# Layer 1 of a two-layer graph network: masks on 64x64 tiles, six two-head steps on VectorE, and a group's divisions three steps apart

## The chip, the cores and the metric

The kernel runs on one core of one Trainium2 chip. The metric is the device time of one execution in microseconds (us). Five engines of the core matter: TensorE (PE in the profile, its weight loads PEld), VectorE (DVE), ScalarE (ACT), GpSimd (POOL) and SyncE (SP), which here only issues transfers. Each engine works through its own queue in order; they meet at semaphores.

## What is computed

Layer 0 is dense attention with an additive bias taken from the adjacency matrix. Layer 1, which the change concerns, is a graph attention with 8 heads of 64 features over 4096 nodes. Cut to what matters:

```python
h = relu(layernorm(x))
nX = per_head_layernorm((h @ W).reshape(n, 8, 64)).transpose(1, 0, 2)
at1 = einsum('kno,ok->kn', nX, a1)[:, :, None]
at2 = einsum('kno,ok->kn', nX, a2)[:, :, None]
kg = leaky_relu(at1 + at2.transpose(0, 2, 1), 0.2) * graph      # 8 x 4096 x 4096
mg = where(mask, kg, -32768.0)
y = softmax(mg, -1) @ nX + nX
x = x + elu(y.transpose(1, 0, 2).reshape(n, 512))
```

`graph` is the float matrix and `mask` says where it is not zero. Both belong to a node pair and are the same for all heads.

## The kernel before

**Tiling of layer 1.** All is held transposed: sources on the 128 partitions, targets in the free dimension. A *group* is 512 targets (`ic`, 8 of them) times four heads (`hg`, 2 of them): 16 groups. A group walks over the sources in 32 *steps* of 128 (`jt`), so there are 512 steps. Four steps share one set of loads, a *block* (`JB = 4`). A step handles four heads of 128 x 512 logits each: heads 0 and 1 are one PSUM tile of two banks (`pair[0]`), heads 2 and 3 another (`pair[1]`). These tiles have the tag `d` and rotate over three buffers; two further banks, `acc0` and `acc1`, hold the group's sums.

**One step** n goes through these functions, with the engine and the line of the profile:

- `z_sums` (PE): four small matmuls with six contracted rows each, on row tiles of 32, put the two-sided logit into PSUM (L1069); then four matmuls of the identity with `ng`, the bf16 mask tile (0 or -2^60), add the mask to each head (L1074). The order is heads 2, 3, 0, 1.
- `relu` (ACT, L1081) makes part of the leaky relu of heads 0 and 1.
- `leaky` (DVE): two `scalar_tensor_tensor` on heads 3 and 2 (L1091), one product with the graph values g (L1096) for the heads that VectorE multiplies itself, and one addition for heads 0 and 1 (L1097). VectorE multiplies head 3 alone, or heads 2 and 3 in a step that is in the set `light`.
- `weigh` (POOL, L1104): the product with g for the other three heads, or for two in a step of `light`.
- `exponent` (ACT, L1107): exp of all four heads.
- `values` (PE, L1120): the weights times the features, on two column tiles of 64. The last column of the features is ones, which gives the softmax sum.

The loop runs them skewed: in iteration n come `values(n - 4)`, `exponent(n - 3)`, `leaky(n)`, `weigh(n)`, `z_sums(n + 1)`, `relu(n + 1)`. The logit tile `t` has six buffers.

**A group's end.** When `values` has done jt = 31, `finish` spreads the rest of the group over the next group's iterations, by a list of offsets d from the iteration n (which is 3 modulo 32) and a place in it: `copies` (ACT, PSUM sums to SBUF, L1136), `to_rows(hf)` (PE, eight records per half, L1142, into one more tile of tag `d`), `divide(hf)` (DVE: reciprocal L1151, product L1153, addition of `own` into `y` L1154), then on ACT `minus`, `exps`, `positive`, `less_one`, and on POOL `elu` (L1178) and `close` (L1182), whose result is stored. `own` (the features that are added) and `xi` (the residual) are loaded by `load_rows`.

**Order.** A call wrapped in `seq` keeps its place in its engine's queue as the program writes it. Row loads and output stores are not wrapped; the framework places them. `load_adj(q)` issues a block's loads on SP: `z2` (128 KB), `nb` (the masks, 512 KB) and `g` (1 MB), two buffers each. In the first group the last 512 rows are still being prepared for layer 1 (`make_ready`), and in the first four groups POOL makes `own` once each (L365, L366).

Of the kernel before, what the change touches and what calls it, by code (L numbers as in the profile page):

```python
# [10 lines left out]
F32 = mybir.dt.float32  # L11
BF16 = mybir.dt.bfloat16
# [6 lines left out]
P = 128  # L19
N = 4096  # L20
D = 512
NH = 8
HD = 64
NB = N // P
SB = 4
# [10 lines left out]
GC = 512  # L36
# [42 lines left out]
def fast_path(  # L79
# [18 lines left out]
    nc = tc.nc  # L98
    seq = tc.keep_in_program_order
# [13 lines left out]
    const = ctx.enter_context(tc.tile_pool(name="const", bufs=1))  # L113
# [4 lines left out]
    ident_b = const.tile([P, P], BF16, name="ident_b")  # L118
# [24 lines left out]
    nT_d = dram.tile([NB, P, N], BF16, name="nT_d")  # L143
# [30 lines left out]
        return mv  # L174


    aa = [const.tile([P, NH, HD], F32, name=f"a{e}_sb") for e in (1, 2)]
    aln_sb = const.tile([P, HD], F32, name="aln_sb")
    bln2_sb = const.tile([P, HD], F32, name="bln2_sb")
    at_b = const.tile([P, 2, NH], F32, name="at_b")  # L180
# [284 lines left out]


    with tc.tile_pool(name="early", bufs=2) as early, tc.tile_pool(name="kv", bufs=1) as kv:
        v = kv.tile([P, NB, D], F32, name="v")
        TILES = [(ic, jt) for ic in range(NI) for jt in range(NB)]
        n_tiles = len(TILES)  # L470
# [66 lines left out]
        with tc.tile_pool(name="proj_c", bufs=1) as pc, tc.tile_pool(  # L537
            name="proj", bufs=2
# [216 lines left out]
            for k in range(KC):  # L755
                pa_ps = psum.tile([P, 512], F32, name="pa", tag="mm", bufs=2)
                for c in range(SB):
                    seq(nc.tensor.matmul(
                        pa_ps, turned["q"][:, c, ts(k, P)], turned["k"][:, c, :],
                        start=c == 0, stop=c == SB - 1,  # L760
# [10 lines left out]
            for sb in range(1, NS):  # L771
                if sb + 2 < NS:
                    xts[sb + 2] = load_x(sb + 2)
                if sb == 1:
                    seq(nc.sync.dma_start(
                        out=w1_sb.rearrange("p k h e -> p k (h e)"),
                        in_=w1.rearrange("(k p) o -> p k o", p=P),
# [23 lines left out]
        with tc.tile_pool(name="attn", bufs=2) as work, tc.tile_pool(  # L801
            name="attn_ps", bufs=2, space=PSUM
# [142 lines left out]
            for s in range(0, n_tiles, 2):  # L945
                ic, jt = TILES[s]
# [48 lines left out]
    with tc.tile_pool(name="ga_in", bufs=2) as inputs, tc.tile_pool(  # L995
# [4 lines left out]
        JB = 4  # L1000
# [3 lines left out]
        inverses = gat.tile([P, NI, 2, 2, 2, 4], F32, name="inverses")  # L1004
        loads, logits, zs, groups = {}, {}, {}, {}

        light = {n + d for n in range(NB + 3, n_steps, NB) for d in (9, 10)}
        later = {}

        def load_adj(q):  # L1010
            ic, _, jt = STEPS[q * JB]
            z2 = inputs.tile([P, JB * P], BF16, name="z2", tag="z2", bufs=2)
            seq(nc.sync.dma_start(
                out=z2, in_=z2_d[:, STEPS[q * JB][1], jt * P : (jt + JB) * P]
            ))
            ng = inputs.tile([P, JB, GC], BF16, name="nb", tag="nb", bufs=2)
            seq(nc.sync.dma_start(
                out=ng, in_=nT_d[jt : jt + JB, :, ts(ic, GC)].rearrange("t p i -> p t i")
            ))
            g = adjs.tile([P, JB, GC], F32, name="g", tag="g", bufs=2)  # L1020
            seq(nc.sync.dma_start(
                out=g, in_=gT_d[jt : jt + JB, :, ts(ic, GC)].rearrange("t p i -> p t i")
            ))
            loads[q] = (g, ng, z2)

        def cols(ic, hg):
            rows = slice(ic * GC, (ic + 1) * GC)
# [32 lines left out]
        def z_sums(n):  # L1060

            ic, hg, jt = STEPS[n]
            _, ng, z2 = loads[n // JB]
            pair = [None, None]
            for hf in (1, 0):
                pair[hf] = psum.tile([P, 2, GC], F32, name="d", tag="d", bufs=3)
            for hh in (2, 3, 0, 1):
                rows = slice(32 * hh, 32 * hh + 6)
                seq(nc.tensor.matmul(  # L1069
                    pair[hh // 2][:, hh % 2, :], z2[rows, ts(jt % JB, P)],  # L1070
                    groups[ic, hg]["z1"][rows, :], start=True, stop=False,
                ))
            for hh in (2, 3, 0, 1):
                seq(nc.tensor.matmul(  # L1074
                    pair[hh // 2][:, hh % 2, :], ident_b, ng[:, jt % JB, :], start=False, stop=True
                ))
            zs[n] = pair

        def relu(n):
# [45 lines left out]
        def finish(n, ic, hg):  # L1125

            grp = groups.pop((ic, hg))
            ob = work.tile([P, 2, GC], F32, name="ob", tag="ob", bufs=1)
            y = work.tile([P, 2, SB * 2, HD], F32, name="y", tag="y", bufs=1)

            def room():
                grp["e"] = work.tile([P, 2, SB * 2, HD], F32, name="e", tag="ob", bufs=1)

            def copies():
                for hf in range(2):
                    seq(nc.scalar.copy(ob[:, hf, :], grp["acc"][hf]))  # L1136

            def to_rows(hf):
                pt = psum.tile([P, 2, GC], F32, name="pt1", tag="d", bufs=3)
                for b in range(SB):  # L1140
                    col = (b % 2) * 2 * HB
                    seq(nc.tensor.matmul(  # L1142
                        pt[:, b // 2, col : col + 2 * HB], ob[:, hf, ts(b, P)],
                        back.rearrange("p e c -> p (e c)"), start=True, stop=True,
                    ))
                grp["pt"] = pt[:, :, 0 : 4 * HB].rearrange("p k (q c) -> p k q c", c=HB)

            def divide(hf):
                v = grp.pop("pt")
                rinv = inverses[:, ic, hg, hf]  # L1150
                seq(nc.vector.reciprocal(rinv, v[:, :, :, HD]))  # L1151
                v = v[:, :, :, 0:HD]
                seq(nc.vector.tensor_mul(v, v, rinv.unsqueeze(3).to_broadcast([P, 2, 4, HD])))  # L1153
                seq(nc.vector.tensor_add(  # L1154
                    y[:, hf].rearrange("p (k q) e -> p k q e", k=2), v,
                    grp["own"][:, hf].rearrange("p b d -> p (b d)")
                    .rearrange("p (k q e) -> p k q e", k=2, e=HD),
                ))

            def flat(t):  # L1160
                return t.rearrange("p f q e -> p (f q e)")

            def minus(hf):
                seq(nc.scalar.activation(grp["e"][:, hf], y[:, hf], AF.Relu, scale=-1.0))

            def exps(hf):
                e = grp["e"][:, hf]
                seq(nc.scalar.activation(e, e, AF.Exp, scale=-1.0))

            def positive():  # L1170
                seq(nc.scalar.activation(flat(y), flat(y), AF.Relu))

            def less_one():
                seq(nc.scalar.add(flat(grp["e"]), flat(grp["e"]), -1.0))

            def elu():
                e = flat(grp["e"])
                seq(nc.gpsimd.tensor_add(e, e, flat(y)))  # L1178

            def close():  # L1180
                e = grp["e"]
                seq(nc.gpsimd.tensor_add(  # L1182
                    flat(e), flat(e), grp["xi"].rearrange("p f b d -> p (f b d)")
                ))
                for f, ap in enumerate(pair_rows(out, ic, hg)):
                    nc.sync.dma_start(
                        out=ap, in_=e[:, f].rearrange("p (b h) e -> p b (h e)", h=2)
                    )

            for d, place, f in (  # L1190
                (0, "mid", copies),
                (1, "mid", lambda: to_rows(0)), (1, "end", lambda: divide(0)),
                (2, "mid", lambda: to_rows(1)), (2, "end", lambda: divide(1)),
                (4, "end", room), (4, "end", lambda: minus(0)), (5, "end", lambda: minus(1)),
                (6, "end", lambda: exps(0)), (6, "end", positive), (7, "end", lambda: exps(1)),
                (8, "end", less_one),
                (9, "end", elu), (10, "end", close),
            ):
                later.setdefault((n + d, place), []).append(f)

# [30 lines left out]
            for f in later.pop((n, place), []):  # L1231
                f()

        for n in range(n_steps + 15):

            q = n // JB + 1
            if n == 1:
                store_rows(NI - 1, last_rows)
            if n % JB == (2 if q == NS - 1 else 0) and q < n_steps // JB:
                load_adj(q)  # L1240
                if q < NS:
                    load_features(q)
            if n < n_steps and STEPS[n][2] == 12:
                load_rows(n)
            if n + 10 < n_steps and STEPS[n + 10][2] == 0:
                open_group(n + 10, nc.sync)
            extra(n, "top")
            if 0 <= n - 4 < n_steps:
                values(n - 4)
                if n % JB == 3:  # L1250
                    loads.pop((n - 4) // JB)
                if STEPS[n - 4][2] == NB - 1:
                    finish(n, *STEPS[n - 4][:2])
            if 0 <= n - 3 < n_steps:
                exponent(n - 3)
            extra(n, "mid")
            for f in left.pop(n, []):
                f()
            if n % JB == 2 and n // JB < NS:
                ones_in(n // JB)  # L1260
            if n < n_steps:
                leaky(n)
                weigh(n)
            if n + 1 < n_steps:
                z_sums(n + 1)
                relu(n + 1)
            for f in left_late.pop(n, []):
                f()
            extra(n, "end")
# [425 lines left out]
```

## Time and profile before

| | |
|---|---|
| median of 3 runs | 3948.41 us (3947.27 to 3952.65) |
| the profiled execution, its own time | 3951.69 us |
| its span | 3949.9 us |
| mean granted TensorE clock | 0.99 |
| busy: PE, DVE, ACT, POOL | 3767.2, 2912.2, 1820.1, 2589.2 us |
| first and last `weigh` of layer 1 (POOL, L1104) | begins 2082.33, ends 3926.25 us |
| 1536-wide and 1024-wide `weigh`, mean | 3501 and 2407 ns in the stretch 2200 to 3900 us |

The span begins with the first instruction; layer 0 fills it up to about 2070 us and layer 1 the rest. Shares of busy time are means over both layers, so layer 1 has to be read from its own stretch. An instruction is listed with its start and its duration; two that follow without a wait on one engine often overlap by some 0.08 us in the records, so the *pitch*, from one start to the next, says more than the duration.

### The profile page before, as it was taken

How to read it: one execution, taken by the hardware profiler on the slowest of the kernel's cores; microseconds unless marked ns; L12 is line 12 of the kernel's file. 1: busy time of each engine (PE TensorE's matmuls, PEld its weight loads, DVE VectorE, ACT ScalarE, POOL GpSimd, SP SyncE). 2: the span in 40 equal slices, each digit the busy share in tenths (PEclk: the TensorE clock that was granted, in tenths of full speed). 3: DMA queues.
4: the chain of work that ended last, by engine and by line, in shares of the span. 5: the costliest groups of instructions: out<-in, count | busy, mean ns of one | idle time of the engine just before them, and what ended most of it. 6: DMA issues, size and time to landing. Idle time of an engine off the chain costs nothing. (4 is left out here: it accounts for less than half of the span.)

```text
span 3949.9 us, 45153 instructions
## 1 busy us (share of the span) xinstructions
PE 3767.2 (95%) x15754; PEld 1862.5 (47%) x15754; DVE 2912.2 (74%) x4420; ACT 1820.1 (46%) x1613; POOL 2589.2 (66%) x1373
## 2 busy tenths in 40 slices
PE   7999999999999999999998899999999999999997
PEld 6876666666666666666653222222222222222222
DVE  5655556565565656566556799999999999999996
ACT  2101011111111111111115788888888888888887
POOL 5432125252341525234247999999999999999998
PEclk9999999999999999999998999999999999999999
DMA  6576657668585866768557544444444444444342
GB/s 203 190 232 202 195 159 219 191 183 223 173 232 150 235 174 205 212 185 220 153 159 189 150 138 146 139 145 138 144 141 146 140 146 145 145 138 146 128 151 80
DMA packets 554414, 670.46 MB, mean 170 GB/s; under 512 B 79808, under 2 KB 397504, under 8 KB 534720
## 3 DMA queue, kind: packets, MB, share of 16 engines
q1 hardware_dynamic: 552112, 665.70, 56.6%
q8 instruction: 126, 2.06, 0.2%
q10 hardware_dynamic: 2064, 1.77, 0.2%
q14 instruction: 112, 0.92, 0.1%
HBM read 495.12 MB, written 172.23 MB: 169 GB/s over the span
## 5 line engine op out<-in xcount | busy, mean ns | idle before, releaser
L1104 POOL TENSOR_TENSOR t<-t,g 128x1536 f32<-128x1536 f32 (+1 forms) x512 | 1723.2, 3434 | 37.4 <-DMA z<-z_d 22.2
L1120 PE MATMUL acc<-t,nX 128*64 128x512 f32 x4096 | 995.3, 607 | 67.2 <-ACT t L1107 54.7
L856 POOL TENSOR_TENSOR total<-total,aT 128x512 f32<-128x512 f32 x248 | 339.5, 1369 | 1063.3 <-ACT aT L851 1056.5
L1107 ACT ACTIVATE t<-t 128x2048 f32<-128x2048 f32 x512 | 975.9, 1906 | 86.4 <-POOL t L1104 85.3
L866 PE MATMUL acc<-v,aT 128*128 128x512 f32 x2048 | 962.5, 592 | 0.0
L851 ACT ACTIVATE aT<-aT 128x512 f32<-128x512 f32 x256 | 161.2, 630 | 1318.6 <-DVE aT L846 1318.6
L1081 ACT ACTIVATE t<-d 128x1024 f32<-128x1024 f32 x512 | 524.8, 1025 | 230.4 <-PE d L1074 226.8
L1097 DVE TENSOR_TENSOR t<-t,d 128x1024 f32<-128x1024 f32 x512 | 620.2, 1211 | 11.2 <-ACT t L1081 11.2
L1074 PE MATMUL d<-nb,ident_b 128*128 128x512 bf16 x2048 | 536.2, 385 | 1.8 <-DMA nb<-nT_d 1.8
L1120 PEld LDWEIGHTS acc<-t,nX 128*64 128x64 f32 x4096 | 250.2, 136 | 595.7 <-issue 340.3
L866 PEld LDWEIGHTS acc<-v,aT 128*128 128x128 f32 x2048 | 389.6, 190 | 273.7 <-issue 245.7
L1091 DVE SCALAR_TENSOR_TENSOR d<-u,at2m,d 128x512 f32<-128x512 f32 x542 | 407.2, 751 | 51.6 <-PE d L1074 36.8
L846 DVE TENSOR_TENSOR aT<-aT,X 128x256 f32<-128x256 f32 x512 | 214.8, 419 | 280.1 <-PE X L838 276.8
L1091 DVE SCALAR_TENSOR_TENSOR t<-u,at2m,d 128x512 f32<-128x512 f32 x482 | 360.0, 747 | 49.6 <-DVE d L1091 1.4
L846 DVE TENSOR_TENSOR aT<-aT,Z 128x256 f32<-128x256 f32 x384 | 159.5, 415 | 293.5 <-PE Z L838 289.0
L1096 DVE TENSOR_TENSOR t<-d,g 128x512 f32<-128x512 f32 (+1 forms) x512 | 366.2, 715 | 5.7 <-DMA g<-gT_d 2.8
L830 DVE SCALAR_TENSOR_TENSOR gs<-ng,aT 128x512 f32<-128x512 bf16 x256 | 285.9, 1117 | 9.8 <-DMA gT_d<-gs 1.1
L1069 PEld LDWEIGHTS <-z 6*128 6x128 bf16 x2048 | 76.4, 91 | 444.0 <-issue 439.9
L1069 PE MATMUL d<-z,z 6*128 6x512 bf16 x2048 | 250.0, 385 | 35.6 <-DVE t L1096 15.8
L1074 PEld LDWEIGHTS <-ident_b 128*128 128x128 bf16 x2048 | 159.3, 98 | 242.3 <-issue 122.7
L838 PE MATMUL Z<-qt,hS 128*128 128x256 f32 x1024 | 264.9, 381 | 8.9 <-DVE aT L846 8.3
L838 PE MATMUL X<-qt,hS 128*128 128x256 f32 x1024 | 264.2, 381 | 0.0
(205 smaller groups left out, 3277.5 us busy)
## 6 DMA issues: line engine op xcount, KB each, us to landing
g<-gT_d SPq DMA_DIRECT2D x128, 1024.0 KB, 5.5
ag<-in_adj_dram SPq DMA_DIRECT2D x256, 256.0 KB, 5.6
hT<-h_d SPq DMA_DIRECT2D x64, 1024.0 KB, 5.9
hS<-s_d SPq DMA_DIRECT2D x64, 1024.0 KB, 8.2
gT_d<-gs SPq DMA_DIRECT2D x256, 256.0 KB, 2.9
nb<-nT_d SPq DMA_DIRECT2D x128, 512.0 KB, 5.2
nT_d<-ng SPq DMA_DIRECT2D x256, 128.0 KB, 3.3
z<-z_d SPq DMA_DIRECT2D x143, 128.0 KB, 4.8
```

The costliest lines, as they stand in the source:

```text
L838: seq(nc.tensor.matmul(out, a, b, start=start and k == 0, stop=k == 1, skip_group_check=not start,))
L846: seq(nc.vector.tensor_add(p, p, part))
L856: seq(nc.gpsimd.tensor_add(totals[ic], totals[ic], p))
L866: seq(nc.tensor.matmul(sums[ic][b], probs[s][:, ts(b, P)], v[:, jt, :], start=jt == 0, stop=jt == NB - 1))
L1074: seq(nc.tensor.matmul(pair[hh // 2][:, hh % 2, :], ident_b, ng[:, jt % JB, :], start=False, stop=True))
L1081: seq(nc.scalar.activation(t[:, 0:2, :], zs[n][0], AF.Relu, scale=4.0))
L1091: seq(nc.vector.scalar_tensor_tensor(pair[1][:, e, :] if e > 1 - mine else t[:, 2, :], u4[:, e, :], at2m[:, jt, h : h + 1], pair[1][:, e, ...
L1096: seq(nc.vector.tensor_mul(t[:, HG - mine : HG, :], pair[1][:, 2 - mine : 2, :], g))
L1097: seq(nc.vector.tensor_add(t[:, 0:2, :], t[:, 0:2, :], pair[0]))
L1104: seq(nc.gpsimd.tensor_mul(t[:, 0:mine, :], t[:, 0:mine, :], g))
L1107: seq(nc.scalar.activation(logits[n], logits[n], AF.Exp))
L1120: seq(nc.tensor.matmul(grp["acc"][hf][ts(e, HD), :], nX[jt // SB][:, jt % SB, hg * HG + 2 * hf + e, :], t[:, 2 * hf + e, :], start=jt == 0 ...
```

## The change

Five edits, all for layer 1:

1. The mask of a head is no longer added by one matmul of the full identity but by two or, seen from the array, four at once for two heads: 64x64 blocks of the identity against 64 rows of the mask. A block that writes the other half of the partitions than the one that it reads needs the mask with its halves swapped, `nx`; two further loads a block bring it (256 KB each).
2. `light` has six steps of every 32 (1, 9, 14, 15, 20, 26), in all 16 groups, where it had two of every 32 from the second group on (12 and 13).
3. The second `to_rows` and `divide` of a group's end come three iterations after the first, not one; all that follows comes two iterations later.
4. `y` has no tile of its own: `divide` adds into `own`. `load_rows` is called at step 20 of a group, not 12. The loop's end is three iterations longer.
5. The tiles `aa` of layer 0 move to a pool that is closed before layer 1.

```diff
-    aa = [const.tile([P, NH, HD], F32, name=f"a{e}_sb") for e in (1, 2)]
+    aa = []
...
     with tc.tile_pool(name="early", bufs=2) as early, tc.tile_pool(name="kv", bufs=1) as kv:
+        aa.extend(kv.tile([P, NH, HD], F32, name=f"a{e}_sb") for e in (1, 2))
...
-        light = {n + d for n in range(NB + 3, n_steps, NB) for d in (9, 10)}
+        light = {n for n in range(n_steps) if n % NB in (1, 9, 14, 15, 20, 26)}
...
+            nx = inputs.tile([P, JB, GC], BF16, name="nx", tag="nx", bufs=2)
+            for r in range(2):
+                seq(nc.sync.dma_start(
+                    out=nx[ts(r, HD)],
+                    in_=nT_d[jt : jt + JB, ts(1 - r, HD), ts(ic, GC)].rearrange("t p i -> p t i"),
+                ))
             g = adjs.tile([P, JB, GC], F32, name="g", tag="g", bufs=2)
...
-            loads[q] = (g, ng, z2)
+            loads[q] = (g, (ng, nx), z2)
...
-            for hh in (2, 3, 0, 1):
-                seq(nc.tensor.matmul(
-                    pair[hh // 2][:, hh % 2, :], ident_b, ng[:, jt % JB, :], start=False, stop=True
-                ))
+            for first in (2, 0):
+                for r, c in ((0, 0), (1, 1), (0, 1), (1, 0)):
+                    hh, rows = first + r, ts(r, HD)
+                    seq(nc.tensor.matmul(
+                        pair[hh // 2][ts(c, HD), hh % 2, :], ident_b[rows, rows],
+                        masks[r != c][rows, jt % JB, :], start=False, stop=True,
+                    ))
...
-            y = work.tile([P, 2, SB * 2, HD], F32, name="y", tag="y", bufs=1)
+            y = grp["own"].rearrange("p f b (h e) -> p f (b h) e", e=HD)
...
-                seq(nc.vector.tensor_add(
-                    y[:, hf].rearrange("p (k q) e -> p k q e", k=2), v,
-                    grp["own"][:, hf].rearrange("p b d -> p (b d)")
-                    .rearrange("p (k q e) -> p k q e", k=2, e=HD),
-                ))
+                own = y[:, hf].rearrange("p (k q) e -> p k q e", k=2)
+                seq(nc.vector.tensor_add(own, v, own))
...
-                (2, "mid", lambda: to_rows(1)), (2, "end", lambda: divide(1)),
-                (4, "end", room), (4, "end", lambda: minus(0)), (5, "end", lambda: minus(1)),
-                (6, "end", lambda: exps(0)), (6, "end", positive), (7, "end", lambda: exps(1)),
-                (8, "end", less_one),
-                (9, "end", elu), (10, "end", close),
+                (4, "mid", lambda: to_rows(1)), (4, "end", lambda: divide(1)),
+                (6, "end", room), (6, "end", lambda: minus(0)), (7, "end", lambda: minus(1)),
+                (8, "end", lambda: exps(0)), (8, "end", positive), (9, "end", lambda: exps(1)),
+                (10, "end", less_one),
+                (11, "end", elu), (12, "end", close),
...
-        for n in range(n_steps + 15):
+        for n in range(n_steps + 18):
...
-            if n < n_steps and STEPS[n][2] == 12:
+            if n < n_steps and STEPS[n][2] == 20:
                 load_rows(n)
```

More of the change, by code (lines that the diff above doesn't have):

```diff
@@ L1062, in z_sums @@
             ic, hg, jt = STEPS[n]
-            _, ng, z2 = loads[n // JB]
+            _, masks, z2 = loads[n // JB]
             pair = [None, None]
```

## The prediction, made before the changed kernel was run

> **What bounds layer 1 now.** I read the busy time by stretches first, then each engine's order of time, then who waited for whom. Columns of the first view: stretch and its length, then busy time and (x instructions) of PE, PEld, DVE, ACT, POOL, the granted clock, the DMA share and GB/s.
>
> ```profile
> core 0: us, PE busy (x) PEld busy (x) DVE busy (x) ACT busy (x) POOL busy (x), PEclk, DMA share, GB/s
> 3000.00:3200.00 200.00, 190.39 (x940) 57.40 (x938) 188.60 (x239) 170.54 (x130) 200.00 (x62) 1.00 0.44 139
> ```
>
> POOL is busy for all of the 200 us; PE and DVE are at 94-95%. The order of time of POOL alone gives its period:
>
> ```profile
> 2737.06 2.39 POOL L1178 TENSOR_TENSOR e<-e,y 128x1024 f32<-128x1024 f32 x1
> 2739.39 2.39 POOL L1104 TENSOR_TENSOR t<-t,g 128x1024 f32<-128x1024 f32 x1
> 2741.71 2.40 POOL L1182 TENSOR_TENSOR e<-e,xi 128x1024 f32<-128x1024 f32 x1
> 2744.05 105.12 POOL L1104 TENSOR_TENSOR t<-t,g 128x1536 f32<-128x1536 f32 x31
> 2849.13 2.36 POOL L1178 TENSOR_TENSOR e<-e,y 128x1024 f32<-128x1024 f32 x1
> ```
>
> From one `elu` to the next are 112.07 us without a gap: 30 wide products at a pitch of 3.43, two of two heads at 2.33, `elu` and `close` at 2.34 each. So **POOL is the bound**. In the first four groups `own` (1.31 + 1.28 us at L365, L366) adds 2.6: the `elu` of 2281.05 and that of 2625.02 are 3 x 114.7 apart.
>
> Next: how far behind are the others? After a group's end POOL is occupied by `elu` and `close` and the others run at their own pace for a dozen steps:
>
> ```profile
> 2992.00 0.75 DVE L1091 SCALAR_TENSOR_TENSOR t<-u,at2m,d 128x512 f32<-128x512 f32 x1
> 2992.66 0.68 DVE L1096 TENSOR_TENSOR t<-d,g 128x512 f32<-128x512 f32 x1
> 2993.26 1.21 DVE L1097 TENSOR_TENSOR t<-t,d 128x1024 f32<-128x1024 f32 x1
> 2993.32 0.48 PE L1069 MATMUL d<-z,z 6*128 6x512 bf16 x4
> 2993.72 1.04 PE L1074 MATMUL d<-nb,ident_b 128*128 128x512 bf16 x4
> 2994.39 0.75 DVE L1091 SCALAR_TENSOR_TENSOR d<-u,at2m,d 128x512 f32<-128x512 f32 x1
> 2994.69 1.94 PE L1120 MATMUL acc<-t,nX 128*64 128x512 f32 x8
> 2995.25 0.75 DVE L1091 SCALAR_TENSOR_TENSOR t<-u,at2m,d 128x512 f32<-128x512 f32 x1
> ```
>
> DVE's pitches are 0.85 and 0.66 (the two L1091), 0.60 (L1096) and 1.13 (L1097): **3.24 us a step**, back to back. PE needs 0.41 + 0.97 + 1.87 = 3.25, but its small matmuls take 0.48 where they take 0.39 unhindered: heads 0 and 1 wait some 0.08 for the PSUM tile that L1096 releases. So both run in step at 3.24, close under POOL's 3.43. A step of `light` on DVE:
>
> ```profile
> 2958.01 1.54 DVE L1091 SCALAR_TENSOR_TENSOR d<-u,at2m,d 128x512 f32<-128x512 f32 x2
> 2959.66 1.23 DVE L1096 TENSOR_TENSOR t<-d,g 128x1024 f32<-128x1024 f32 x1
> 2960.80 1.21 DVE L1097 TENSOR_TENSOR t<-t,d 128x1024 f32<-128x1024 f32 x1
> 2961.93 0.75 DVE L1091 SCALAR_TENSOR_TENSOR d<-u,at2m,d 128x512 f32<-128x512 f32 x1
> ```
>
> That is 1.65 + 1.14 + 1.13 = 3.92, **0.68 more** than a normal step, for 1.09 off POOL.
>
> [...] This trace agrees for row tiles (four L1069 in 0.41, not 4 x 0.24) and for pairs of column tiles (L1120); it shows no 64x64 pack. [...]
>
> **The change part by part.**
>
> *Masks.* Unknown: a 64x64 pack. The old pitch is 0.97 / 4 = 0.24 for one mask. At best a pack of four lasts one such: 0.49 for the step, 0.48 less. At worst all eight run in turn: 1.94, 0.97 more. I take 0.54, 0.43 less, because row tiles and column tiles each overlap here; [...]. It hides: PE falls to some 2.8 against DVE's 3.24. Its use is slack: the first L1091 could start 0.82 after the end of L1096 instead of 1.04, while DVE needs 1.04 for L1097.
>
> *Six steps of light.* POOL per group: 26 x 3.43 + 6 x 2.33 + 2 x 2.34 = 107.8. DVE: 26 x 3.24 + 6 x 3.92 = 107.8, and the two divisions at 0.24 + 0.74 + 0.61 = 1.59 each: 110.9. **The bound moves to DVE.** With two light steps DVE's sum would be 108.2, so the six cost it 2.7; in the groups with `own` POOL has 110.4, still below.
>
> *Stalls of DVE.* While POOL leads they cost nothing, now they count. Before, a group has 0.54 ahead of the first reciprocal, 0.73 ahead of an L1091 after `exps` and `positive`, and two of about 0.25 on ACT ahead of L1097:
>
> ```profile
> 2926.84 0.21 DVE L1151 RECIPROCAL inverses<-pt 128x8 f32<-128x8 f32 x1 [0.54 <-PE pt L1142]
> 2954.11 1.55 DVE L1091 SCALAR_TENSOR_TENSOR d<-u,at2m,d 128x512 f32<-128x512 f32 x2 [0.73 <-PE d L1074]
> ```
>
> The first goes: `copies` start earlier when exp no longer waits for POOL, and PE's eight L1142 then end about when L1097 does. The second stays in part: `exps` and `positive` hold ACT 0.52 + 0.95, exp comes late, `values` and the next masks with it; the shorter mask gives back 0.2, leaving 0.5. `less_one` falls ahead of light step 15 and hides. Second division: PE has 1.94 + 1.16 us of L1120 and L1142 behind the masks and is done before L1097, no stall. Three steps between divisions let the `d` buffers recover; in before the adjacent ones made PE wait 0.43 for L1097. A group: **111.5**, 0.6 below 112.1, and 3.2 below 114.7 in the four first.
>
> *Sum.* `weigh` of step 26 starts at 2214.43 and the last ends at 3926.25, 1711.8. After: 395 x 3.24 + 90 x 3.92 + 15 x (3.18 + 0.56) = 1688.7 to the last L1097, the last `weigh` 3.4, a lag of POOL of 2.4 (it loses 0.19 in each normal step since 26): 1694.5, **17 less**. The tail behind it keeps its chain.
>
> *Steps 0 to 26 (2076 to 2214).* PE carries 4.7 us of projection per four steps (L292, L300) and POOL waits for it; 0.43 a step from the masks, 1.09 off POOL and 0.68 onto DVE in five steps: about 5 less. At the start L1096 waits 2.77 for g, and `nx` goes ahead of g on SP: 0.5 MB at 200 GB/s or so, 2 more. Together -3, between -8 and +5.
>
> *Transfers.* 128 blocks get two issues (0.4 us of SP each) and 0.5 MB: 64 MB over layer 1, some 36 GB/s on 140, the DMA share 0.44 to about 0.56. `nx` comes free with `nb`, four steps (13 us) ahead of need; `nb` lands in 5.2. Queued behind it on SP are g and the next block. g waits for the last `weigh` of two blocks back, and lands barely a microsecond before its need now (issue 2917.83, 5.5 to land, L1096 at 2924.2); POOL's shorter lag gives room. `load_rows`' four DMAs now follow `elu` and `close`, past later block loads on SP; their need is 20 steps away. Cost zero, at most 1 us a block.
>
> *The rest at nothing:* adding into `own` is the same instruction with another output; ACT's delayed pieces hide in ACT's 0.5 us a step; `aa` only changes its address.
>
> In all 20 less than the profile's own 3951.7: 3931.4. The median stood 3.3 under it: **3928**.
>
> **Rivals.**
>
> *No change.* DVE's stalls reach 1.1 to 2 a group (other pieces of ACT come too late): each 0.1 beyond my 0.56 costs 1.5 us over 15 groups. 3941 to 3956, 0.19. For: ACT-made stalls exist in before. Against: 13 steps without one at 3.24.
>
> *64x64 blocks do not overlap*, slower. In `z_sums`, eight at 0.24: PE 3.25 + 0.97 = 4.2 a step, 136.6 a group with L1142, 24 more than now: 4330. It decides from a mask time of about 1.2 on, where PE passes 3.48 a step, DVE's mean (111.5 / 32); half overlap, 0.97, loses nothing. 0.06. The change would then not do what it says.
>
> *g or nx late*, slower: 0.3 to 1 us a block beyond slack is 40 to 130: 3960 to 4060, 0.08. Light steps dearer than 0.68 with more stalls: 3957 to 3970, 0.03.
>
> *More gain*: no stalls, first steps -8: 3905 to 3915, 0.06 with shorter pitches.
>
> The likeliest, DVE at 111 to 112 a group: 3915 to 3940, 0.58.
>
> **Numbers.** Faster by over 0.2% (below 3940.5; about what a measurement here can tell) 0.64, within 0.2% 0.19, slower 0.17. Range 3905 to 3952: it leaves out the slower rivals (0.17) and little below.
>
> **To be seen after.** Four L1074 of a pack within 0.25 us, masks of a step in 0.5; POOL idle for L1097, 96-97% busy; DVE without gaps at 3.24 and 3.92; `elu` to `elu` 111.5, the first groups too; POOL's wide products 26 a group. Wrong if L1074 keep their 0.24 each, if L1096 waits for DMA, or if `elu` to `elu` stays at 112 with idle time on both DVE and POOL.

## The result, and the profile after

The changed kernel takes **4016.94 us** (median of 4, 4014.37 to 4021.32) against 3949.64 us: **1.7% slower**, ratio 1.0171 with the interval 1.0154 to 1.0189. The forecast was 3928 and a range up to 3952. The profiled execution took 4014.37 us, span 4012.5.

First the busy time in the stretch that was shown of before (columns as there), then the order of time of POOL:

```profile
3000.00:3200.00 200.00, 180.48 (x1130) 49.93 (x1132) 184.81 (x233) 159.81 (x121) 185.60 (x59) 0.97 0.64 179
```

```profile
2874.43 2.36 POOL L1188 TENSOR_TENSOR e<-e,own 128x1024 f32<-128x1024 f32 x1
2879.09 2.37 POOL L1192 TENSOR_TENSOR e<-e,xi 128x1024 f32<-128x1024 f32 x1
...
2990.25 2.37 POOL L1188 TENSOR_TENSOR e<-e,own 128x1024 f32<-128x1024 f32 x1
2994.91 2.38 POOL L1192 TENSOR_TENSOR e<-e,xi 128x1024 f32<-128x1024 f32 x1
```

POOL is no longer full: 93% busy, where 96-97% was forecast. But DVE has fallen to 92%, and nothing else is full either. From one `elu` to the next are 115.8 us here; over the 14 intervals from 2287.92 to 3925.58 the mean is 117.0. The forecast was 111.5; before it was 112.1 (114.7 in the first ones).

A step at its own pace, to be laid beside the one of before:

```profile
2994.24 0.40 PE L1086 MATMUL d<-nb,ident_b 64*64 64x512 bf16 x2
2994.25 0.40 PE L1086 MATMUL d<-nx,ident_b 64*64 64x512 bf16 x2
2994.48 0.38 PE L1086 MATMUL d<-nb,ident_b 64*64 64x512 bf16 x2
2994.49 0.38 PE L1086 MATMUL d<-nx,ident_b 64*64 64x512 bf16 x2
2994.80 1.94 PE L1133 MATMUL acc<-t,nX 128*64 128x512 f32 x8
2994.91 0.75 DVE L1104 SCALAR_TENSOR_TENSOR d<-u,at2m,d 128x512 f32<-128x512 f32 x1
2995.77 0.75 DVE L1104 SCALAR_TENSOR_TENSOR t<-u,at2m,d 128x512 f32<-128x512 f32 x1
2996.43 0.68 DVE L1109 TENSOR_TENSOR t<-d,g 128x512 f32<-128x512 f32 x1
2997.03 1.21 DVE L1110 TENSOR_TENSOR t<-t,d 128x1024 f32<-128x1024 f32 x1
2998.16 0.75 DVE L1104 SCALAR_TENSOR_TENSOR d<-u,at2m,d 128x512 f32<-128x512 f32 x1
```

Four 64x64 matmuls (two of `nb`, two of `nx`) start within 0.01 us, the next four 0.24 later, and `values` 0.56 after the first: the pack works, with the 0.54 that was taken. DVE's pitches are still 0.86, 0.66, 0.60 and 1.13, 3.25 from 2994.91 to 2998.16. Eight microseconds further on in the same group, PE's and DVE's lines with what ended the idle time before them:

```profile
3005.90 0.40 PE L1086 MATMUL d<-nb,ident_b 64*64 64x512 bf16 x2 [1.50 <-DMA nb<-nT_d]
3007.16 0.37 PE L1086 MATMUL d<-nx,ident_b 64*64 64x512 bf16 x1 [0.86 <-DMA nx<-nT_d]
3008.39 0.58 PE L1086 MATMUL d<-nx,ident_b 64*64 64x512 bf16 x1 [0.85 <-DMA nx<-nT_d]
...
3009.00 1.55 DVE L1104 SCALAR_TENSOR_TENSOR d<-u,at2m,d 128x512 f32<-128x512 f32 x2 [3.92 <-PE d L1086]
3009.32 3.10 PE L1133 MATMUL acc<-t,nX 128*64 128x512 f32 x8
```

The masks of step 20 come late from HBM, and DVE stands for 3.92 us. The groups before and after have the same stall, of 3.49 and 2.46 us; after 2200 us PE waits 15 times for `nb` and 30 times for `nx`, once and twice a group. Why, the order of time of SP alone tells:

```profile
2972.95 0.34 SPq L1015 DMA_DIRECT2D z<-z_d  x1
...
2980.61 0.36 SPq L1030 DMA_DIRECT2D g<-gT_d  x1
2992.65 0.92 SPq L1066 DMA_DIRECT2D own<-own_d  x2
2993.62 0.49 SPq L1043 DMA_DIRECT2D z<-z_d  x1
2994.16 0.98 SPq L1046 DMA_DIRECT2D u<-u_d  x2
2997.31 0.93 SPq L1196 DMA_DIRECT2D out_dram<-e  x2
2998.33 0.58 SPq L1015 DMA_DIRECT2D z<-z_d  x1
2999.01 1.01 SPq L1019 DMA_DIRECT2D nb<-nT_d  x1
3000.11 1.24 SPq L1025 DMA_DIRECT2D nx<-nT_d  x2
```

SP issues nothing from 2981 to 2992.65. Next in its queue is the load of `own`, which since the change waits for `elu` (its end is 2990.25 + 2.37 = 2992.62). Behind it come `z1` and `u4` of the next group (L1043, L1046) and the stores of the output, which wait for `close` (2994.91 + 2.38 = 2997.29). Behind those stands the block that `load_adj` issues in iteration 16, for steps 20 to 23. Its mask buffer was free when the masks of step 15 were done, at 2987.7; `nb` goes out at 2999.0, eleven microseconds late, and is wanted at 3004.3. `z1` and `u4` are written at step 22 and wrapped in `seq`, and yet they go out ahead of the block of step 16: the order of a queue has to be read from the profile, not from the program. The same place before the change, first SP, then the masks of steps 15 and 20 on PE:

```profile
2846.87 0.36 SPq L1021 DMA_DIRECT2D g<-gT_d  x1
2856.18 0.91 SPq L1057 DMA_DIRECT2D xi<-x_d  x2
2857.18 1.01 SPq L1186 DMA_DIRECT2D out_dram<-e  x2
2858.28 0.55 SPq L1013 DMA_DIRECT2D z<-z_d  x1
2858.91 0.59 SPq L1017 DMA_DIRECT2D nb<-nT_d  x1
```

```profile
2852.47 1.04 PE L1074 MATMUL d<-nb,ident_b 128*128 128x512 bf16 x4
...
2868.71 1.04 PE L1074 MATMUL d<-nb,ident_b 128*128 128x512 bf16 x4
```

SP waited there for `close` too (2853.78 + 2.36 = 2856.14), but `close` came two steps earlier. The masks of step 15 end at 2853.5 and `nb` goes out at 2858.9, 5.4 us late; 9.8 us were left to step 20, and `nb` took 5.2 to land at the median. More than half of the slack was already spent, and no engine's wait showed it.

### The profile page after: what moved, and what is told of

It reads as the page before. It is cut to its first block, busy times and chain, and to the rows that moved or that the text cites. A ratio compares the mean times of both kernels' runs of the same rounds, so it can differ in the third digit from the quotient of the medians.

```text
span 4012.5 us, 49644 instructions
## 1 busy us (share of the span) xinstructions
PE 3711.3 (92%) x17802; PEld 1803.6 (45%) x17802; DVE 2937.8 (73%) x4420; ACT 1802.6 (45%) x1613; POOL 2524.1 (63%) x1373
## 5 line engine op out<-in xcount | busy, mean ns | idle before, releaser
L1117 POOL TENSOR_TENSOR t<-t,g 128x1536 f32<-128x1536 f32 (+1 forms) x512 | 1656.7, 3268 | 168.3 <-DVE t L1110 137.2
L1133 PE MATMUL acc<-t,nX 128*64 128x512 f32 x4096 | 1019.1, 619 | 45.7 <-ACT t L1120 40.6
L1120 ACT ACTIVATE t<-t 128x2048 f32<-128x2048 f32 x512 | 975.5, 1906 | 1.2 <-POOL t L1117 1.2
L1104 DVE SCALAR_TENSOR_TENSOR d<-u,at2m,d 128x512 f32<-128x512 f32 x608 | 455.6, 749 | 99.6 <-PE d L1086 96.1
L1078 PE MATMUL d<-z,z 6*128 6x512 bf16 x2048 | 372.2, 389 | 127.2 <-DVE t L1109 76.6
L1109 DVE TENSOR_TENSOR t<-d,g 128x512 f32<-128x512 f32 (+1 forms) x512 | 401.2, 784 | 22.1 <-DMA g<-gT_d 13.2
L1078 PEld LDWEIGHTS <-z 6*128 6x128 bf16 x2048 | 93.1, 91 | 649.0 <-issue 376.8
L1086 PE MATMUL d<-nx,ident_b 64*64 64x512 bf16 x2048 | 333.3, 397 | 25.8 <-DMA nx<-nT_d 25.8
L1086 PE MATMUL d<-nb,ident_b 64*64 64x512 bf16 x2048 | 327.9, 396 | 25.6 <-DMA nb<-nT_d 25.6
L1104 DVE SCALAR_TENSOR_TENSOR t<-u,at2m,d 128x512 f32<-128x512 f32 x416 | 310.6, 747 | 43.6 <-DVE d L1104 1.4
```

The source lines that it names most:

```text
L1078: seq(nc.tensor.matmul(pair[hh // 2][:, hh % 2, :], z2[rows, ts(jt % JB, P)], groups[ic, hg]["z1"][rows, :], start=True, stop=False,))
L1086: seq(nc.tensor.matmul(pair[hh // 2][ts(c, HD), hh % 2, :], ident_b[rows, rows], masks[r != c][rows, jt % JB, :], start=False, stop=True,))
L1104: seq(nc.vector.scalar_tensor_tensor(pair[1][:, e, :] if e > 1 - mine else t[:, 2, :], u4[:, e, :], at2m[:, jt, h : h + 1], pair[1][:, e, ...
L1109: seq(nc.vector.tensor_mul(t[:, HG - mine : HG, :], pair[1][:, 2 - mine : 2, :], g))
L1117: seq(nc.gpsimd.tensor_mul(t[:, 0:mine, :], t[:, 0:mine, :], g))
L1120: seq(nc.scalar.activation(logits[n], logits[n], AF.Exp))
```

## The experiments

Theory A: the place on SP. Loads and stores that wait for POOL stand ahead of a block's loads and make them late; what they set free then goes out in one burst. Rivals: B, the new wait of `own` alone; C, the 0.5 MB of `nx` a block, whatever the order; D, light steps dearer than 0.68 us; E and F below. A burst here means several loads issued within a few microseconds. Each run is compared with the kernel before on the same chip; a ratio's interval is 95%. On the chips used the kernel before took 3946.95 to 3951.77 us, so a difference between two runs can be off by some us.

**1. Rows in their written order.** The loads of `own` and `xi` are held at step 20.

```diff
-                    nc.sync.dma_start(out=t[:, f], in_=ap)
+                    seq(nc.sync.dma_start(out=t[:, f], in_=ap))
```

> The changed kernel with the loads of own and xi held at their written place, step 20, behind the block load of that step on SP; the output stores stay where they are, ahead of the block load of step 16, and still wait for close. Theory A (the stores' wait for close is what makes the block's masks late): the block is issued as late as before (12 us), only half a MB less stands ahead of it, so the stall of VectorE shrinks from about 4.5 to 2.5 to 4 us a group: 3975 to 4005 us. Rival B (the wait of own for elu makes them late): the stall goes, 3925 to 3945. Rival C (the 0.5 MB of nx a block is too much for the DMA engines, whatever the order): no change, 4010 to 4020.

Measured: 3992.19 us, ratio 1.0104 (1.0088 to 1.0121). As A says: 25 us go, but the block still goes out behind the stores and DVE's waits for masks are still there, up to 3.6 us. The edit moved more than the rows: `z1` and `u4`, too, now go out behind the blocks of steps 16 and 20. So the 25 us belong to `own`, `z1` and `u4` together.

**2. Stores behind the block as well.** In addition:

```diff
-                    nc.sync.dma_start(
+                    seq(nc.sync.dma_start(
...
-                (11, "end", elu), (12, "end", close),
+                (11, "end", elu), (12, "end", close), (14, "end", store),
```

> As the last, and the output stores are issued two steps later (offset 14 in place of 12), behind the block load of step 16 on SP. Theory A: no block load stands behind a wait for POOL any more, VectorE sets the pace at some 111.5 us a group with its one stall of 0.5, elu to elu 111 to 112.5: 3920 to 3945 us. Rival B: the same as the run with the rows alone. Rival C: 3990 to 4020, with waits of the mask matmuls on DMA left in every block.

Measured: 3977.14 us, ratio 1.0066 (1.0049 to 1.0083). Better by 15 more, but not the 3920 to 3945 that A promised. The order of SP and DVE in this run shows what is left:

```profile
2892.39 0.38 SPq L1019 DMA_DIRECT2D nb<-nT_d  x1
2892.86 3.01 SPq L1025 DMA_DIRECT2D nx<-nT_d  x2
...
2897.47 0.36 SPq L1030 DMA_DIRECT2D g<-gT_d  x1
...
2909.76 0.69 DVE L1109 TENSOR_TENSOR t<-d,g 128x512 f32<-128x512 f32 x1 [1.50 <-DMA g<-gT_d]
```

`xi`, `own`, `z1`, `u4` and the block's own loads go out between 2885 and 2898, and g takes 12 us to land, where its median in the changed kernel is 5.6. Moving the rows behind step 20 had put them beside `open_group` of step 22.

**3. Without nx.** The two loads go, and the crossed blocks read the unswapped mask; what is added there is another sources' mask.

```diff
-            nx = inputs.tile([P, JB, GC], BF16, name="nx", tag="nx", bufs=2)
-            for r in range(2):
...
-            loads[q] = (g, (ng, nx), z2)
+            loads[q] = (g, (ng, ng), z2)
```

> The changed kernel without the two loads of nx: the crossed 64x64 blocks read the unswapped mask, so the mask added there is that of other sources; all instructions stay. SP's order and waits stay. Theory A: the block is issued just as late, but 0.5 MB less is in flight and nothing comes 1.2 us behind nb: the stall falls by 1.5 to 3 us a group, 3965 to 3995 us. Rival C (volume of nx): the stall goes wholly, 3920 to 3940, and g's time to land falls too.

Measured: 3959.54 us, ratio 1.0027 (1.0015 to 1.0038). With SP's order nearly untouched (only `xi` goes out one block earlier) 57 us go, a little more than A said and less than C: the bytes of `nx` matter where the block is late. DVE still waits for g once a group, 1.2 us on average and 2.1 at most. Bytes and lateness act together, so what runs take back singly does not add up.

**4. Edit 4 alone, on the kernel before.** `divide` adds into `own`, `load_rows` at step 20.

> The kernel before with one part of the change: divide adds into own, y has no tile, and load_rows is called at step 20. The stores keep their place. On SP the load of own now waits for elu, just ahead of the stores that wait for close. Theory A: close comes after elu, so the wait of own adds nothing; POOL stays the bound, 3943 to 3956 us. Rival B: the block behind it comes late, 2 to 5 us a group, 3975 to 4025.

Measured: 3948.21 us, ratio 1.0000 (0.9991 to 1.0008). Rival B falls: where `close` is early and no `nx` follows, the wait of `own` costs nothing, although `z1` and `u4` come ahead of the block here too.

**5. The single loads spread.** On run 2:

```diff
-            if n < n_steps and STEPS[n][2] == 20:
-                load_rows(n)
-            if n + 10 < n_steps and STEPS[n + 10][2] == 0:
-                open_group(n + 10, nc.sync)
+            if n < n_steps and STEPS[n][2] == 18:
+                load_rows(n, "own", own_d)
+            if n < n_steps and STEPS[n][2] == 30:
+                load_rows(n, "xi", x1_d)
+            if n + 6 < n_steps and STEPS[n + 6][2] == 0:
+                open_group(n + 6, nc.sync)
```

> As the run with rows and stores in order, and the group's single loads are spread: own at step 18, xi at step 30, z1 and u4 of the next group at step 26 in place of 22. What was left there: rows (1 MB), u4 and z1 (0.6 MB) and a block of 2.1 MB were issued within 10 us, and g landed 12 us after its issue; L1109 waited 1.5 to 1.8 us for it and the masks some more. Theory A (the burst): the waits on g go, elu to elu 111.5 to 112.5 in place of 114.5 to 115.5, 3928 to 3952 us. Rival C (nx's volume delays g in every block): no change, 3968 to 3985.

Measured: **3936.79 us, ratio 0.9970 (0.9961 to 0.9980)**. All five edits are in it (of the fourth all but the step of `load_rows`), and the 64 MB of `nx`; 80 us have come back by place and time of issue alone. Rival C falls as a cause by itself. DVE has one stall of note left in a group, the one that the prediction kept:

```profile
2950.05 1.55 DVE L1104 SCALAR_TENSOR_TENSOR d<-u,at2m,d 128x512 f32<-128x512 f32 x2 [0.50 <-PE d L1086]
```

`elu` to `elu` is 111.7 in nearly all groups, 112.0 and 112.1 in the first two.

**6 and 7. Light steps alone, on the kernel before**: six (1, 9, 12, 13, 20, 26), then four (1, 12, 13, 22).

> The kernel before with six light steps alone (1, 9, 12, 13, 20, 26: elu and close stay in light steps), full masks, no nx, divisions one step apart. Theory A: VectorE leads with 110.9 us a group and its own stalls, 0.54 + 0.73 + 0.5, so 112.2 to 113: no longer 2.6 more in the first four groups: 3942 to 3962 us. Rival D (a light step costs VectorE more than 0.68 once it leads): 3965 to 4000.

> The kernel before with four light steps (1, 12, 13, 22), nothing else. POOL: 28 x 3.43 + 4 x 2.33 + 4.7 = 110.0 us a group, VectorE 28 x 3.24 + 4 x 3.92 + 3.2 = 109.6 and stalls of 1 to 1.8. Theory A: 110.5 to 111.5 a group, 3918 to 3938 us. Rival D: no gain, 3945 to 3960.

Measured: six 3950.35 us, ratio 1.0003 (0.9994 to 1.0011), 112.7 a group; four **3934.35 us, ratio 0.9962 (0.9948 to 0.9976)**, 111.6 a group and 112.6 where POOL makes `own`. Both times are in A's bands; the group of the run with four is 0.1 above its own. Rival D falls: 0.68 holds as the price of a light step, and six are two too many. Six alone bring nothing.

**8. Masks with two light steps.** Run 2 with `light` at 14 and 15 alone.

> The run with rows and stores in order, but with two light steps a group (14 and 15, from the second group on), so masks on 64x64, nx, and the later divisions without the shift of work to VectorE. Theory A: POOL leads again with 112.1 us, VectorE's waits for data hide in its slack: 3944 to 3958 us. Rival C: the loads of nx come late whoever leads: 3965 to 3985.

Measured: 3966.40 us, ratio 1.0041 (1.0027 to 1.0055), out of A's band by 8. In two groups DVE waits 1.9 and 2.5 us for g, and 2.2 and 1.2 for masks ahead of it; PE waits for `nx` 27 times in 14 groups. POOL's lead doesn't hide that. The time lies in C's band; but the waits are not in every block, as C would have them, and run 5 has none with the same `nx`. A had underrated the burst here as in run 2.

**9. The best of both.** Run 5 with four light steps, five in the first five groups.

```diff
-        light = {n for n in range(n_steps) if n % NB in (1, 9, 14, 15, 20, 26)}
+        light = {
+            n for n in range(n_steps)
+            if n % NB in ((1, 9, 14, 15, 22) if n < 5 * NB else (1, 14, 15, 22))
+        }
```

> The run with spread loads, with four light steps a group (1, 14, 15, 22), five in the first five groups (and 9), where POOL also makes own. POOL: 28 x 3.43 + 4 x 2.33 + 4.7 = 110.0, VectorE 28 x 3.24 + 4 x 3.92 + 3.2 + 0.5 = 110.1. Theory A (VectorE's sum of pitches set 111.7 with six): 110.2 to 110.8 a group, some 112 in groups 1 to 4: 3914 to 3930 us. Rival E (111.7 comes from something else, such as PE or the loads): no change, 3933 to 3942.

Measured: **3922.37 us, ratio 0.9940 (0.9924 to 0.9957)**, faster than both kernels; 110.0 to 110.7 a group, 111.5 with `own`. Rival E falls.

**10. The same with full masks and no nx.**

> As the last, but with the full masks of before, one matmul of the identity a head, and no nx. Theory A: the 64x64 masks take 0.5 us a step from PE, which is not the bound; they save VectorE only part of its one stall (0.73 against 0.5) and 0.3 of another: 110.6 to 111.3 a group, 3918 to 3936 us, at most 10 slower than the last. Rival F (the masks' slack carries the gain): back to 112 or more, 3940 to 3955.

Measured: 3934.10 us, ratio 0.9968 (0.9956 to 0.9979), 111.7 a group. The time is in A's band, but the group is 0.4 above it, and 12 us are lost where A allowed 10; F's 112 is not reached. So the 64x64 masks are worth 12 us when their loads come in time, about half of run 9's gain: DVE's stalls of 0.7, 0.4 and 0.3 a group are back (sums of 10.2, 5.6 and 3.8 us over 14 groups).

**11. Stores early again.** Run 5, with `store` back at offset 12.

> The run with spread loads and six light steps, with the output stores back at offset 12, so that they wait for close ahead of the block load of step 16 on SP. Theory A: that block is issued some 10 to 12 us late with 5 us left until its need; without the rows' and u4's bytes in flight it lands 0.5 to 3 us late: 112.2 to 114.7 a group, 3945 to 3985 us. If late issue costs only with a burst behind it: 3933 to 3942.

Measured: 3986.48 us, ratio 1.0102 (1.0086 to 1.0119), 114.1 to 116.2 a group. SP waits for `close` and the block is issued late, with no rows or `u4` in flight ahead of it:

```profile
2966.72 0.37 SPq L1030 DMA_DIRECT2D g<-gT_d  x1
2983.43 0.93 SPq L1198 DMA_DIRECT2D out_dram<-e  x2
2984.45 0.49 SPq L1015 DMA_DIRECT2D z<-z_d  x1
2985.04 0.60 SPq L1019 DMA_DIRECT2D nb<-nT_d  x1
```

Two stores at that place cost 50 us, slightly more than A's band. Lateness needs no burst.

**12. The offsets undone, in the changed kernel.** Divisions one step apart, `elu` and `close` in steps 12 and 13, which replace 14 and 15 in `light`; all else as changed, the rows' and stores' order too.

> The changed kernel with one part undone: the divisions one step apart again and all offsets behind them as before, so that elu and close fall in steps 12 and 13, which take the place of 14 and 15 in the set of light steps. Rows and stores are left to the framework and their written places as in the change. Theory A (the later close is what makes the block behind the stores late): close ends two steps, 6.5 us, earlier, the block of step 16 is issued some 6 us late in place of 12, and the masks come in time or less than 1 us late; own's load and u4's stay in the way of g: 112 to 114.5 a group, 3942 to 3980 us. If the later close plays no part: 4005 to 4020.

Measured: 3954.97 us, ratio 1.0008 (1.0000 to 1.0017). Undoing edit 3, with the two light steps that go with it, takes back 62 of the 67 us. The masks' matmuls no longer wait for a DMA in the profile. What stays is a stall of DVE of 2.1 us in six of the 14 groups, which take 113.3 to 113.8 us, where the others have 0.54 at the same place and take 111.8 to 112.5. The granted clock tells them apart: PE waits 1.21 us for exp ahead of `values` in both, but in the six the clock falls just after (to 0.50 from 2957 to 2959 in the group shown), and `values` takes 3.1 us or more. One group without and one with:

```profile
2843.68 1.94 PE L1133 MATMUL acc<-t,nX 128*64 128x512 f32 x8 [1.21 <-ACT t L1120]
2846.39 1.55 DVE L1104 SCALAR_TENSOR_TENSOR d<-u,at2m,d 128x512 f32<-128x512 f32 x2 [0.54 <-PE d L1086]
...
2955.43 3.08 PE L1133 MATMUL acc<-t,nX 128*64 128x512 f32 x8 [1.21 <-ACT t L1120]
2959.74 1.55 DVE L1104 SCALAR_TENSOR_TENSOR d<-u,at2m,d 128x512 f32<-128x512 f32 x2 [2.14 <-PE d L1086]
```

## Why the prediction was wrong

**Right, by its steps.** POOL was the bound before, and the bound moved to DVE. The pack of 64x64 blocks (0.56 for 0.54; the 0.54 was an estimate from the profile of before, where four L1069 take 0.41 on row tiles, and L1120's eight matmuls of 0.59 on column tiles start two at a time, 0.47 from pair to pair). A light step's 0.68 (runs 6, 7 and 9: two light steps fewer in run 9 gave 1.2 us a group). The stall after `exps` and `positive` fell from 0.73 to 0.50, to the digit. The period, 111.5 forecast, is 111.7 in run 5; its profiled execution took 3935.33 us against a sum of 3931.4.

**Right by luck.** The stall ahead of the reciprocal is gone in run 5, but not for the reason given, that exp no longer waits for POOL: in run 6, where DVE leads, 0.4 of it stays, and in run 10, which differs from run 9 in the masks and `nx` alone, it is back (0.4 at most). The shorter masks took it away; the prediction counted them as slack and 0.2 of another stall, and they are worth 12 us.

**Wrong, one step: "Transfers".** It took the moved `load_rows` at "Cost zero, at most 1 us a block" because "their need is 20 steps away". That asks what the moved transfer needs and not what stands behind it. It also put these loads "past later block loads on SP"; the profile shows `own`, and `z1` and `u4` with it, ahead of the block. In the listing of the changed kernel SP issues in order: `own`, which nobody wants for 60 us, holds all behind it while it waits for `elu`, and nothing goes out from 2981 to 2992.65. Of the stores the step said nothing, though `close` comes two steps later, and they weigh more: 50 us in run 11. The numbers were in the profile of before: SP idle from 2846.87 to 2856.18, then the stores, then a block 5.4 us late with 9.8 us left. `close` two steps on is 6.5 more, which is above the 4.6 by which 9.8 exceeds the 5.2 that `nb` takes. In the changed kernel 5.3 us were left, for an `nb` that now has `nx` behind it and a burst ahead of it. The prediction looked at the slack of g, and took `nb` and `nx` as free "four steps ahead of need" without asking whether SP could issue them then. The added bytes themselves came as forecast (179 GB/s, against 139 + 36), at a DMA share of 0.64 for the 0.56 taken. The 200 GB/s taken for the first `nx` was a rough estimate: the kernel before moved 190 from 2060 to 2090 us.

The rival "g or nx late" had the sign and the size, 3960 to 4060, but only 0.08, and named no mechanism on SP. Nor did the later divisions bring much: with full masks a group takes 111.6 with them one step apart (run 7) and 111.7 with three (run 10); undoing them with their two steps of delay gave back 4.4 us a group (117.0 in the changed kernel, 112.6 in run 12), eight times the stall of 0.54 ahead of the reciprocal that was to go.

In the group from 2990.25 to 3106.66 the excess is all on DVE: beside the stall of 0.50 that was forecast it has 0.46, 3.92 and 0.44. These 4.8 us and the 111.5 make 116.3, and 116.4 were measured. Other groups took up to 119.0 and were not added up. How much each of `own`, `xi`, `z1` and `u4` has in the burst stays open; run 5 moved them together.

## To carry to other kernels

When an edit delays a result, look up every transfer that waits for it, and then what is queued behind that transfer on its issuing engine: a store may not be urgent, but the load behind it may be. Read the issuing queue's idle time ahead of a load whose buffer is free as slack that is already spent, even when no engine waits for it yet. And when work is balanced by moving it between two engines, sum the pitches of both for each possible split before taking one: here 4 steps, not 6.

## What the runs showed of the hardware

In some stretches behind a wait TensorE's granted clock was halved, to 0.50, for some 3 us. The busy time by stretches of the changed kernel, ahead of the stall at 3004 to 3008, in it and behind it:

```profile
2990.00:3000.00 10.00, 9.41 (x63) 2.47 (x62) 9.34 (x12) 8.15 (x7) 10.00 (x5) 1.00 0.52 142
3007.00:3008.00 1.00, 0.37 (x1) 0.10 (x1) 0.00 (x0) 0.00 (x0) 1.00 (x2) 1.00 1.04 313
3009.00:3010.00 1.00, 1.00 (x6) 0.29 (x4) 0.96 (x2) 0.51 (x1) 1.00 (x1) 0.50 1.08 359
3012.00:3013.00 1.00, 1.00 (x14) 0.24 (x12) 1.00 (x2) 0.31 (x1) 0.00 (x0) 1.00 1.14 229
```

The granted clock is 0.50 at 3009 and 1.00 again at 3012, and the eight matmuls of `values` at 3009.32 last 3.10 us instead of 1.94. Ahead of that PE had a few matmuls only for about 4 us, 0.77 us of busy time from 3005 to 3008. In run 12 the same follows a gap of 1.21 us in some groups, and in others, and in run 5 (1.22 us), such a gap leaves the clock at 1.00. So here the length of the gap alone does not decide; what else does stays open. In run 12 the groups with a halved clock cost DVE 2.14 - 0.54 = 1.6 us more, behind a wait of PE of 1.21 us: more than the wait's own length.

Over the whole span the mean clock was 0.979 in the changed kernel and 0.990 before and in runs 5 and 9. In stretches of 2 us from 2280 to 3880 it fell below 0.95 at 14 places in the changed kernel, and nowhere before or in runs 4, 5, 6, 7, 9 and 10.
